# Turning the residual stream by DMA in the out projection instead of by TensorE in the feed-forward stage, with the feed-forward rounds in a new order

## The chip, the cores and the metric

The kernel runs on one core of a Trainium2 chip. The metric is device time in microseconds (us). The kernel before took 2558.52 us, the median of 3 runs (2558.04 to 2558.9). A profiled execution of it took 2555.83 us. A run with several rounds alternates both kernels on the same chip.

In what follows PE is TensorE, PEld its weight load, DVE is VectorE, ACT is ScalarE, POOL is GpSimd, and SP is SyncE, which here only issues transfers.

## The reference

A block of a transformer over 64 x 64 tokens with 1024 features, all in float32 but for two roundings to bfloat16. In short:

```python
# x: (64, 64, 1024); the second axis is the attention's sequence
y  = einsum("bct,bcd->bdt", x, cond_weights[itok_B_0_15])      # a 64x64 mix of positions per sequence
x1 = x + attention(y, qkvw, qkvb, ow, ob)                      # 32 heads of 32, softmax, out projection

base   = x1 @ W.T                                              # 1024 x 1024
logits = x1 @ Wr.T + 5 * one_hot(itok_B_0_7)                   # 8 experts
gates  = softmax over the two largest logits, 0 elsewhere
z      = base + 2 * sum over experts of gates * (x1 @ A.T) @ B.T    # LoRA of rank 16 per expert

q, s   = quantize(bf16(z) * inv)      # per token: s = max|.|/127, q = clip(round(./s), -127, 127)
inter  = bf16(clip(silu(gate) * up, -10, 10))    # gate, up: q @ w.T * s * w_scale, 512 wide
out    = x1 + (quantize(inter * inv_inter) @ w_down.T) * scales
```

Two products take x1: the router with the LoRA's first factor (8 x 17 = 136 columns), and the base (1024 columns). For a matmul on PE both need x1 with features on partitions, that is turned.

## The kernel before, in words

The 4096 tokens are 32 tiles of 128 tokens; two tiles make a pair, of which there are 16. The kernel has three stages in a row.

*Attention.* Eight blocks of four tiles. The order of work is written out by a small list of due times. Its result is stored per pair in DRAM (`ctx_d`), with features on partitions. In its last phase the first two pairs of the out projection are woven in.

*Out projection* (class `OutProjection`). For each pair, a product of 256 tokens x 1024 features with a 1024 x 1024 weight, by Winograd's variant of Strassen's scheme: seven products in place of eight, in the order 1, 6, 7, 5, 2, 4, 3. Each product is four float32 matmuls of 128 x 512, each issued as two instructions, so that one product is eight rows of the trace and about 3.43 us. `pair(p)` returns the seven steps; each has `product()` (the matmuls) and `rest()` (what reads the result). The PSUM banks are a, b, c, d: products 1 and 2 share a, 7 and 4 share c, 5 and 3 share d. `prepare(p + 1)` makes the four sums of token quarters (To, on DVE) for the next pair, after product 5. POOL adds the bias `ob` to the loaded x (L1092) and the shared sums `ou` (L1106). After product 3 SP stores the two tiles of x1 in the output tensor (L1114), then loads the context (`cx`, L1067) and x (`xo`, L1073) two pairs ahead. Each engine takes its instructions in the order in which they are written, and SP's transfers wait in one line as well: a transfer whose data is not ready holds up all after it.

*Feed-forward stage* (`second_stage`). One round per pair, in which pair p's router, base product and gates are computed, and the quantized gate, up and down products of pairs p-1 and p-2. The order within a round is written out by hand as a list of calls (`router`, `base(p, i)`, `after(p, i)`, `quant_a`, `quant_b`, `gate_or_up`, `scaled`, `glu`, `down`, `result`). Each round begins with `x1_transposed` (L1232, L1233): PE turns the sixteen 128 x 128 blocks of the pair's x1, which was loaded again from the output tensor (L1156), and ACT copies them from PSUM to SBUF. `quant_a` quantizes on DVE and ACT, `quant_b` clips and turns the bfloat16 values by a DMA transpose from SP (L1381). `result` adds the scaled down product to the output in DRAM by an accumulating transfer from POOL; only the last three tiles are added in SBUF, to an x1 that is still there, and stored.

The PSUM pool `ps_h` has four banks, taken in turn by `x1_transposed`, `router`, `down`, `gates_transposed` and `gate_or_up`; `ps_g` has four, for the products a to d.

Of the kernel before, what the change touches and what calls it, by code (L numbers as in the profile page):

```python
# [11 lines left out]
F32 = mybir.dt.float32  # L12
BF16 = mybir.dt.bfloat16
I32 = mybir.dt.int32
AF = mybir.ActivationFunctionType
# [4 lines left out]
P = 128  # L20
# [15 lines left out]
def adaln_attn_ffn(ctx: ExitStack, tc: tile.TileContext, a, out: bass.AP):  # L36
# [26 lines left out]

    I = a["w_gate_t"].shape[1]
# [9 lines left out]
    with tc.manual_schedule(), ExitStack() as psum, ExitStack() as early:  # L74
        ps_g = psum.enter_context(tc.tile_pool(name="ps_g", bufs=4, space=PSUM, reuse_waits="tile"))
        st = early.enter_context(tc.tile_pool(name="halve", bufs=2))
        chores = halve_weights(tc, st, const, dram, srcs, half, any_i)
        chores = itertools.chain(chores, combine_quarters(tc, st, (("wo", a["ow"]), ("wt", a["w_t"])), comb))
        op = OutProjection(tc, a, x_t, out_t, ctx_d, ps_g, comb, KC, H)
        attention(tc, a, x_t, ctx_d, ident, dram, ps_g, KC, PB, NBLK, NCH, HPC, H, C, chores, early, op)  # L80
        second_stage(tc, a, out_t, ident, ps_g, KC, NT, H, C, half, comb, op)

    inexact = nc.values_load(any_i[0:1, 0:1], min_val=0, max_val=1)
    with tc.If(inexact != 0):
        feed_forward(tc, a, x_t, out_t, ctx_d, ident, KC, NT, PB, H, C, None)

# [946 lines left out]
class OutProjection:  # L1033


    def __init__(self, tc, a, x_t, out_t, ctx_d, ps_g, comb, KC, H):
        self.tc, self.a, self.x_t, self.out_t, self.ctx_d, self.ps_g, self.comb = tc, a, x_t, out_t, ctx_d, ps_g, comb
        self.KC, self.H = KC, H
        self.NPAIR = len(ctx_d)
        self.stack = ExitStack()  # L1040
        self.st = {}
# [15 lines left out]
    def open_rest(self):  # L1057
        self.xp, self.tp, self.up = self.pool("xo3", 2), self.pool("to3", 2), self.pool("uo3", 1)
        self.load_x(0)
        self.load_ctx(1)  # L1060
        self.load_x(1)
        self.prepare(0)
# [17 lines left out]

    def pair(self, p):
# [5 lines left out]
        def one(i):  # L1087
# [8 lines left out]
            def rest():  # L1096
                x, ps = self.st[p]["x"], u.pop(("ps", i))
                if i in (1, 6, 7):
                    u[i] = self.up.tile([P, HH], F32, tag=f"u{i}", name=f"ou{i}_{p}")
                    if i == 1:  # L1100
                        nc.scalar.copy(u[1], ps)  # L1101
                    else:
                        nc.vector.tensor_tensor(u[i], ps, u[1 if i == 6 else 6], ALU.add)  # L1103
                    if i == 7:
                        for t, n, v in ((1, 1, u[7]), (0, 1, u[6]), (1, 0, u[6])):
                            nc.gpsimd.tensor_tensor(x[:, t, hs[n]], x[:, t, hs[n]], v, ALU.add)  # L1106
                    return
                t, n = {5: (1, 1), 2: (0, 0), 4: (0, 1), 3: (1, 0)}[i]
                nc.vector.tensor_tensor(x[:, t, hs[n]], ps, x[:, t, hs[n]], ALU.add)
# [14 lines left out]
def second_stage(tc, a, out_t, ident, ps_g, KC, NT, H, C, half, comb, op):  # L1124
# [12 lines left out]
    with ExitStack() as ctx:  # L1137
# [33 lines left out]
        for p in range(2, NPAIR):  # L1171
# [6 lines left out]
            if p == NPAIR - 3:  # L1178
                first_loads()
        op.stack.close()  # L1180
# [44 lines left out]
        def x1_transposed(p):  # L1225
            s = st[p]
            s["xT"] = p1p.tile([P, 2, KC, P], F32, tag="xT", name=f"xT_{p}")
            for t in range(2):
                for q in range(0, KC, 4):
                    ps = ps_h.tile([P, 4, P], F32, tag="h", name=f"xTp_{p}_{t}_{q}")  # L1230
                    for c in range(4):
                        nc.tensor.transpose(ps[:, c, :], s["x"][:, t, (q + c) * P:(q + c + 1) * P], ident)  # L1232
                    nc.scalar.copy(s["xT"][:, t, q:q + 4, :], ps)  # L1233
# [194 lines left out]
        def result(p, t, adds=None):  # L1428
# [3 lines left out]
            for n in range(2):  # L1432
# [3 lines left out]
                if adds:  # L1436
                    adds.tensor_add(y[:, hs[n]], y[:, hs[n]], s["x"][:, t, hs[n]])
# [11 lines left out]
        for p in range(NPAIR - 1):  # L1449
            q, r = p - 1, p - 2  # L1450
            old, last = q >= 0, r >= 0
            x1_transposed(p)
# [12 lines left out]
            do(old, quant_a, q, 0, "u")  # L1465
# [37 lines left out]
        x1_transposed(p)  # L1503
# [3 lines left out]
        quant_a(r, 1, "i")  # L1507
# [3 lines left out]
        quant_b(r, 1, "i")  # L1511
        base(p, 1)
        after(p, 1)
        route(p)
        result(r, 0)
        base(p, 6)
        gates_transposed(p)
# [112 lines left out]
```

## Time and profile before

| | |
|---|---|
| median of 3 runs | 2558.52 us (2558.04 to 2558.9) |
| the profiled execution | 2555.83 us |
| its span, first to last instruction | 2554.0 us |
| TensorE clock granted | 0.996 |
| attention, up to 1430 us | 1430 us, PE busy 1413.59 |
| attention's last phase with pairs 0 and 1, 1430 to 1487 us | 57 us, PE busy 55.26 |
| out projection, 1487 to 1830.4 us | 343.4 us, PE busy 343.40 |
| feed-forward, 1830.4 to 2554 us | 723.6 us, of which PE is idle mostly in the last 39 (busy 18.5) |

A row of the profile has the line, the engine, the operation, what it writes and reads (buffer numbers left out), and the number of instructions. In a timeline a row starts with the start in us from the span's start and the time that the row takes; a bracket at its end tells how long the engine was idle before and what it waited for. The number before "us to landing" of a transfer counts from its issue to its data's arrival. Times of matmuls are from issue to a modelled end, so that successive matmuls overlap in the table.

### The profile page before, as it was taken

How to read it: one execution, taken by the hardware profiler on the slowest of the kernel's cores; microseconds unless marked ns; L12 is line 12 of the kernel's file. 1: busy time of each engine (PE TensorE's matmuls, PEld its weight loads, DVE VectorE, ACT ScalarE, POOL GpSimd, SP SyncE). 2: the span in 40 equal slices, each digit the busy share in tenths (PEclk: the TensorE clock that was granted, in tenths of full speed). 3: DMA queues.
4: the chain of work that ended last, by engine and by line, in shares of the span. 5: the costliest groups of instructions: out<-in, count | busy, mean ns of one | idle time of the engine just before them, and what ended most of it. 6: DMA issues, size and time to landing. Idle time of an engine off the chain costs nothing.

```text
span 2554.0 us, 35008 instructions
## 1 busy us (share of the span) xinstructions
PE 2512.6 (98%) x13955; PEld 1779.0 (70%) x14000; DVE 1569.1 (61%) x2957; ACT 631.1 (25%) x1111; POOL 366.0 (14%) x451
## 2 busy tenths in 40 slices
PE   8999999999999999999999999999999999999996
PEld 7888888888888888888888644444454545455452
DVE  4575575674664655654745734434367777777777
ACT  1132231221221222322312200000033334343433
POOL 5110001011112221110000233434200000000001
PEclk9999999999999999999999999999999999999998
DMA  8664545555556546544443444443524344434333
GB/s 271 241 229 133 193 162 191 173 168 177 184 161 211 182 155 207 184 152 156 141 137 153 164 166 162 167 164 124 194 75 77 81 77 78 84 69 86 71 52 72
DMA packets 207885, 378.10 MB, mean 148 GB/s; under 512 B 96098, under 2 KB 150371, under 8 KB 196067
## 3 DMA queue, kind: packets, MB, share of 16 engines
q1 hardware_dynamic: 177202, 309.19, 37.1%
q0 software_dynamic: 12080, 49.82, 7.4%
q10 hardware_dynamic: 18432, 16.79, 1.9%
q8 instruction: 112, 1.84, 0.3%
q14 instruction: 59, 0.48, 0.1%
HBM read 271.40 MB, written 83.89 MB: 139 GB/s over the span
## 4 chain that ended last, share of the span: by engine, by line
PE 94%; DVE 3%; DMA 1%; ACT 0%; issue 0%; SPq 0%; DVEq 0%
PE pska L419 4%; PE pskd L419 4%; PE pskc L419 4%; PE psqa L419 4%; PE pod L995 4%; PE pbc L995 4%; PE pba L995 4%; PE psqd L419 4%; PE psvd L446 4%; PE psva L446 4%; PE psqc L419 4%; PE poa L995 4%; PE poc L995 4%; PE psvc L446 4%; PE pbd L995 4%; PE s L482 3%
## 5 line engine op out<-in xcount | busy, mean ns | idle before, releaser
L494 DVE TENSOR_REDUCE mx<-s 128x8 f32<-128x512 f32 x128 | 88.1, 689 | 138.5 <-PE s L482 137.4
L516 ACT COPY pT<-pt 128x512 f32<-128x512 f32 x128 | 75.0, 586 | 318.1 <-PE pt L514 318.1
L405 DVE SCALAR_TENSOR_TENSOR kbd<-pskd,bqkv,psku 32x256 f32<-32x256 f32 x256 | 122.8, 480 | 35.6 <-PE pskd L419 32.2
L536 ACT ACTIVATE co<-c,bqkv 128x256 f32<-128x256 f32 x128 | 60.6, 473 | 338.7 <-PE c L526 312.8
L1092 POOL TENSOR_TENSOR xo<-xo,ob 128x1024 f32<-128x1024 f32 x32 | 87.5, 2753 | 306.8 <-DMA xo<-in_x_dram 306.8
L419 PE MATMUL psqa<-yB,wq 128*128 128x256 f32 x512 | 123.5, 384 | 0.0
L419 PE MATMUL pska<-yB,wk 128*128 128x256 f32 x512 | 122.7, 383 | 0.0
L1441 POOL DMA_DIRECT2D out_dram<-y x29 | 25.1, 864 | 680.4 <-DVE y L1433 680.4
L446 PE MATMUL psva<-wv,yB 128*128 128x256 f32 x512 | 116.6, 381 | 0.0
L995 PE MATMUL poa<-woA,cx 128*128 128x512 f32 x256 | 115.3, 593 | 0.0
L995 PE MATMUL pba<-wtA,xT 128*128 128x512 f32 x256 | 115.1, 592 | 0.0
L498 ACT ACTIVATE prob<-prob 128x512 f32<-128x512 f32 x128 | 78.9, 628 | 108.1 <-DVE prob L495 81.5
L446 PEld LDWEIGHTS psva<-wv,yB 128*128 128x128 f32 x512 | 96.1, 190 | 12.9
L419 PEld LDWEIGHTS pska<-yB,wk 128*128 128x128 f32 x512 | 94.1, 190 | 12.2
L419 PEld LDWEIGHTS psqa<-yB,wq 128*128 128x128 f32 x512 | 92.8, 190 | 12.0 <-issue 0.2
L1106 POOL TENSOR_TENSOR xo<-xo,ou 128x512 f32<-128x512 f32 x48 | 59.4, 1266 | 249.4 <-DVE ou L1103 249.4
L506 DVE TENSOR_TENSOR prob<-prob,den 128x512 f32<-128x512 f32 x128 | 91.0, 711 | 4.4
L405 DVE SCALAR_TENSOR_TENSOR kbd<-pskc,bqkv,psku 32x256 f32<-32x256 f32 x128 | 61.5, 481 | 51.3 <-PE pskc L419 49.9
L495 DVE TENSOR_TENSOR prob<-s,mx 128x512 f32<-128x512 f32 x128 | 88.5, 691 | 4.4
L504 DVE TENSOR_REDUCE den<-prob 128x8 f32<-128x512 f32 x128 | 86.6, 677 | 7.0 <-ACT prob L498 6.8
L1101 ACT COPY ou<-poa 128x512 f32<-128x512 f32 x16 | 9.4, 585 | 327.1 <-PE poa L995 326.7
L995 PEld LDWEIGHTS poa<-woA,cx 128*128 128x128 f32 x256 | 48.4, 190 | 59.9 <-issue 59.8
(244 smaller groups left out, 5276.9 us busy)
## 6 DMA issues: line engine op xcount, KB each, us to landing
wv<-v_d SPq DMA_DIRECT2D x98, 512.0 KB, 3.7
wq<-q_d SPq DMA_DIRECT2D x28, 1792.0 KB, 7.9
wk<-k_d SPq DMA_DIRECT2D x28, 1792.0 KB, 8.0
x<-in_x_dram SPq DMA_DIRECT2D x32, 512.0 KB, 9.7
ctx_d<-co ACTq DMA_DIRECT2D x128, 128.0 KB, 5.6
cx<-ctx_d SPq DMA_DIRECT2D x16, 1024.0 KB, 5.9
xo<-in_x_dram SPq DMA_DIRECT2D x32, 512.0 KB, 5.2
out_dram<-xo SPq DMA_DIRECT2D x32, 512.0 KB, 2.7
```

Of the source, the lines that this page charges most:

```text
L405: nc.vector.scalar_tensor_tensor(dst, ps, bias, u, ALU.add, ALU.add)
L419: nc.tensor.matmul(ps[:, 0:HB], A[:, SLOT[A_OF[i]], k, :], B[B_OF[i]][:, k, :], start=first and k == 0, stop=k == KQ - 1, skip_group_check ...
L446: nc.tensor.matmul(ps[:, j * VC:(j + 1) * VC], B[B_OF[i]][:, k, j * P:(j + 1) * P], A[:, k, :], start=first and j == 0 and k == 0, stop=k ...
L482: nc.tensor.matmul(ps[halves[r], hp, n, jj * 2:(jj + 1) * 2, :], q_of[b, c][halves[hp], m, t * HB + t0:t * HB + t0 + C], kbd[u][halves[hp] ...
L494: nc.vector.tensor_reduce(mx_v, ps, AX.X, ALU.max)
L495: nc.vector.tensor_tensor(p.rearrange("p (a e) k -> p a e k", a=2), ps, mx_v.unsqueeze(3).to_broadcast([P, 2, HPC, C]), ALU.subtract)
L498: nc.scalar.activation(p, p, AF.Exp, scale=scale)
L504: nc.vector.tensor_reduce(den, p, AX.X, ALU.add)
L506: nc.vector.tensor_tensor(p, p, den.unsqueeze(2).to_broadcast([P, n, C]), ALU.mult)
L516: nc.scalar.copy(pT, pt)
L995: self.nc.tensor.matmul(ps, self.B[self.B_OF[i]][:, k, :], self.A[self.A_OF[i]][:, k, :], start=first and k == 0, stop=k == self.KQ - 1, s ...
L1092: nc.gpsimd.tensor_add(s["x"][:, t, :], s["x"][:, t, :], self.ob)
```

## The change

*In the out projection* each finished tile of x1 is turned in the shadow of the other work. [...]`turn(p, t)` has ACT split half a tile (512 features of float32) into its two 16-bit planes (`planes`, a view of the words as low and high halves), and SP turns both planes with one DMA transpose. `turned()`, called later, has ACT weave the turned planes back into float32, and SP stores that in a new DRAM tensor `xT_d[p]`. Tile 0 is turned after product 4 and woven back after product 3; tile 1 is turned after product 3, and woven back after product 6 of the next pair (for the last pair at the stage's end).

*In the feed-forward stage* `x1_transposed` is gone; `load_x1` loads the turned pair as one transfer of 1 MB, at the head of the round before. The last three tiles' x1 is loaded from the output tensor at the head of the last round.

*The rounds' order:* the token sums move ahead of the inner activation's `quant_a`; its `quant_b` moves into the next `quant_a`; `gates_transposed` moves behind product 5, and the first gate product moves ahead of the LoRA matmul of product 5. In the last round product 7 follows product 6.

```diff
+def planes(x):
+    return x.bitcast(I16).rearrange("p (n h) -> p h n", h=2)
...
 class OutProjection:
...
     def open_rest(self):
         self.xp, self.tp, self.up = self.pool("xo3", 2), self.pool("to3", 2), self.pool("uo3", 1)
+        self.hp = self.pool("ho3", 2)
...
+    def turn(self, p, t):
+        nc, n = self.tc.nc, self.H // 2
+        for f in range(2):
+            h = self.hp.tile([P, 2, n], I16, tag="h", name=f"xh_{p}_{t}_{f}")
+            nc.scalar.copy(h, planes(self.st[p]["x"][:, t, f * n:(f + 1) * n]))
+            hT = self.hp.tile([P, 2, n], I16, tag="hT", name=f"xhT_{p}_{t}_{f}")
+            nc.sync.dma_start(
+                hT.rearrange("p h (k q) -> p (h k) q", q=P), h.rearrange("p h n -> p (h n)"), transpose=True
+            )
+            self.turning.append((p, t, f, hT))
+
+    def turned(self):
+        nc, n, KQ = self.tc.nc, self.H // 2, self.KC // 2
+        for p, t, f, hT in self.turning:
+            xT = self.hp.tile([P, KQ, P], F32, tag="xT", name=f"xTo_{p}_{t}_{f}")
+            nc.scalar.copy(planes(xT.rearrange("p k q -> p (k q)")), hT)
+            nc.sync.dma_start(self.xT_d[p][:, t, f * KQ:(f + 1) * KQ, :], xT)
+        self.turning = []
...
             def rest():
                 x, ps = self.st[p]["x"], u.pop(("ps", i))
+                if i in (6, 3):
+                    self.turned()
...
                 if i == 5 and p + 1 < self.NPAIR:
                     self.prepare(p + 1)
+                if i in (4, 3):
+                    self.turn(p, t)
                 if i == 3:
                     for t in range(2):
                         nc.sync.dma_start(self.out_t[2 * p + t], x[:, t, :])
...
         def load_x1(p):
             s = st1[p] = {}
-            s["x"] = xp1.tile([P, 2, H], F32, tag="x", name=f"x1_{p}")
-            for t in range(2):
-                nc.sync.dma_start(s["x"][:, t, :], out_t[2 * p + t])
+            s["xT"] = xp1.tile([P, 2, KC, P], F32, tag="x", name=f"x1T_{p}")
+            nc.sync.dma_start(s["xT"], xT_d[p])
...
+        op.turned()
         op.stack.close()
...
-        def x1_transposed(p):
-            s = st[p]
-            s["xT"] = p1p.tile([P, 2, KC, P], F32, tag="xT", name=f"xT_{p}")
-            for t in range(2):
-                for q in range(0, KC, 4):
-                    ps = ps_h.tile([P, 4, P], F32, tag="h", name=f"xTp_{p}_{t}_{q}")
-                    for c in range(4):
-                        nc.tensor.transpose(ps[:, c, :], s["x"][:, t, (q + c) * P:(q + c + 1) * P], ident)
-                    nc.scalar.copy(s["xT"][:, t, q:q + 4, :], ps)
-            s["B"] = token_quarters(s["xT"], KQ)
-
         def token_sums(p):
             s = st[p]
+            s["B"] = token_quarters(s["xT"], KQ)
...
         for p in range(NPAIR - 1):
             q, r = p - 1, p - 2
             old, last = q >= 0, r >= 0
-            x1_transposed(p)
+            do(p > 0, load_x1, p + 1)
             do(old, after, q, 3)
             do(last, scaled, r, 1, "u")
             do(last, glu, r, 1)
-            do(last, quant_a, r, 1, "i")
             router(p)
             do(last, down, r, 0)
-            do(p + 2 < NPAIR, load_x1, p + 2)
             token_sums(p)
-            do(last, quant_b, r, 1, "i")
+            do(last, quant_a, r, 1, "i")
             base(p, 1)
             after(p, 1)
             do(last, result, r, 0)
-            do(old, quant_a, q, 0, "u")
+            do(old, quant_a, q, 0, "u", (r, 1, "i") if last else None)
             base(p, 6)
             route(p)
             after(p, 6)
             do(old, quant_b, q, 0, "u")
             base(p, 7)
             do(last, down, r, 1)
-            gates_transposed(p)
             do(last, result, r, 1)
             base(p, 5)
+            gates_transposed(p)
             do(old, quant_a, q, 1, "g")
+            do(old, gate_or_up, q, 0, "g")
             lora_5(p)
             after(p, 7)
             after(p, 5)
-            do(old, gate_or_up, q, 0, "g")
...
         p, q, r = NPAIR - 1, NPAIR - 2, NPAIR - 3
-        x1_transposed(p)
+        st[q]["x", 1] = p1p.tile([P, H], F32, tag="xl", name="x1_l")
+        nc.sync.dma_start(st[q]["x", 1], out_t[2 * q + 1])
+        xl = xp1.tile([P, 2, KC, P], F32, tag="x", name="x1_ll").rearrange("p t k n -> p t (k n)")
+        for t in range(2):
+            st[p]["x", t] = xl[:, t, :]
+            nc.sync.dma_start(xl[:, t, :], out_t[2 * p + t])
...
         base(p, 6)
+        base(p, 7)
         gates_transposed(p)
         after(p, 6)
         quant_a(q, 0, "u")
         base(p, 2)
         after(p, 2)
+        after(p, 7)
         quant_a(q, 1, "g", (q, 0, "u"))
         down(r, 1)
         result(r, 1)
-        base(p, 7)
-        after(p, 7)
```

More of the change, by code (lines that the diff above doesn't have):

```diff
@@ L14 @@
 I32 = mybir.dt.int32
+I16 = mybir.dt.int16
 AF = mybir.ActivationFunctionType
@@ L61, in adaln_attn_ffn @@
     ]
+    xT_d = [dram.tile([P, 2, KC, P], F32, tag=f"xT_d{p}", name=f"xT_d{p}") for p in range(NT // 2)]
     I = a["w_gate_t"].shape[1]
@@ L78, in adaln_attn_ffn @@
         chores = itertools.chain(chores, combine_quarters(tc, st, (("wo", a["ow"]), ("wt", a["w_t"])), comb))
-        op = OutProjection(tc, a, x_t, out_t, ctx_d, ps_g, comb, KC, H)
+        op = OutProjection(tc, a, x_t, out_t, ctx_d, xT_d, ps_g, comb, KC, H)
         attention(tc, a, x_t, ctx_d, ident, dram, ps_g, KC, PB, NBLK, NCH, HPC, H, C, chores, early, op)
-        second_stage(tc, a, out_t, ident, ps_g, KC, NT, H, C, half, comb, op)
+        second_stage(tc, a, out_t, xT_d, ident, ps_g, KC, NT, H, C, half, comb, op)
     inexact = nc.values_load(any_i[0:1, 0:1], min_val=0, max_val=1)
@@ L1033, with __init__ @@
 class OutProjection:
-    def __init__(self, tc, a, x_t, out_t, ctx_d, ps_g, comb, KC, H):
+    def __init__(self, tc, a, x_t, out_t, ctx_d, xT_d, ps_g, comb, KC, H):
         self.tc, self.a, self.x_t, self.out_t, self.ctx_d, self.ps_g, self.comb = tc, a, x_t, out_t, ctx_d, ps_g, comb
+        self.xT_d, self.turning = xT_d, []
         self.KC, self.H = KC, H
@@ L1121, in pair, with second_stage @@
         return [one(i) for i in Winograd.ORDER]
-def second_stage(tc, a, out_t, ident, ps_g, KC, NT, H, C, half, comb, op):
+def second_stage(tc, a, out_t, xT_d, ident, ps_g, KC, NT, H, C, half, comb, op):
     nc = tc.nc
@@ L1436, in result @@
                 if adds:
-                    adds.tensor_add(y[:, hs[n]], y[:, hs[n]], s["x"][:, t, hs[n]])
+                    adds.tensor_add(y[:, hs[n]], y[:, hs[n]], s["x", t][:, hs[n]])
                     nc.sync.dma_start(out_t[2 * p + t, :, hs[n]], y[:, hs[n]])
@@ L1506, in second_stage @@
         glu(r, 1)
-        quant_a(r, 1, "i")
         router(p)
@@ L1510, in second_stage @@
         token_sums(p)
-        quant_b(r, 1, "i")
+        quant_a(r, 1, "i")
         base(p, 1)
@@ L1514, in second_stage @@
         route(p)
+        quant_b(r, 1, "i")
         result(r, 0)
         base(p, 6)
+        base(p, 7)
         gates_transposed(p)
```

## The prediction

> **What bounds the kernel now.** I read the page's busy shares and its chain of work first, then the busy time by stage, then the timeline of one feed-forward round and of one out-projection pair.
>
> ```profile
> PE 2512.6 (98%) x13955; PEld 1779.0 (70%) x14000; DVE 1569.1 (61%) x2957; ACT 631.1 (25%) x1111; POOL 366.0 (14%) x451
> ...
> PE 94%; DVE 3%; DMA 1%; ACT 0%; issue 0%; SPq 0%; DVEq 0%
> ```
>
> TensorE (PE) works 98% of the span and is 94% of the chain that ended last: time taken off PE's list is time off the end, unless something new makes PE wait. By stage (columns: stretch, length, then busy time of PE, PEld, DVE, ACT, POOL, clock, DMA share, GB/s):
>
> ```profile
> 1487.00:1830.40 343.40, 343.40 (x802) 152.11 (x801) 152.87 (x141) 8.20 (x14) 128.82 (x72) 1.00 0.41 152
> 2122.00:2471.80 349.80, 348.54 (x1289) 181.77 (x1312) 269.82 (x578) 133.44 (x186) 13.77 (x16) 1.00 0.39 76
> 2515.00:2554.00 39.00, 18.50 (x75) 7.25 (x73) 28.44 (x54) 12.94 (x17) 6.34 (x5) 0.75 0.28 70
> ```
>
> The out projection (first line) has PE busy all the time and ACT nearly idle. In the feed-forward stage (second line) PE idles 1.26 us in eight rounds; DVE is at 77%. Only the last 39 us belong to a DVE and ACT chain. The head of one feed-forward round:
>
> ```profile
> 2122.23 1.91 PE L1232 MATMUL xTp<-ident,x 128*128 128x128 f32 x16
> 2122.87 2.05 ACT L1233 COPY xT<-xTp 128x512 f32<-128x512 f32 x4 [1.65 <-PE xTp L1232]
> 2123.98 3.87 PE L1246 MATMUL pr<-awr,xT 128*128 128x136 f32 x32
> ```
>
> From the first turning matmul to the first router matmul is 2123.98 - 2122.23 = 1.75 us of PE's list. The 1.91 us holds the pipelined end of the last matmul, which hides under the router.
>
> **What the skill says.** The Trainium skill, "TensorE: Matmul & The Clock Gate", Part 4: PE-mode transpose, gives about 275 ns for one 128x128 turn and says the result goes to PSUM, so a copy follows. The trace agrees (273 ns, four copies), but shows that the price in a stream is the spacing, 1.75/16 = 0.11 us, not the latency. "DMA: Bandwidth & Descriptors", DMA Transpose (X-bar), Constraints: 2-byte types only, into SBUF. That is why float32 is split into two 16-bit planes; the transposes of bf16 in this trace have the same number of 16-bit words. "SBUF — State Buffer", Who interferes with whom: DVE and GpSimd share a port pair as an exclusive lock. The trace agrees: sums To take 2.72 and 2.83 us beside POOL's adds, 0.69 us without. The same page, Door 1: The DMA port swizzle, says that a 2-byte operand may stride up to 8 elements at full bandwidth (the planes stride 2); no row here shows a strided 16-bit copy on ACT.
>
> **The change, part by part.** *Removed on PE:* 16 rounds x 16 matmuls at 1.75 us = 28.0 us. In round 1 the router also waited for the ACT copies (1863.95 to 1866.31 = 2.36 us in place of 1.75), so 28.6 us. ACT's four copies per round (2.05 us) go too, but ACT was not the bound.
>
> *Added on ACT and the queues, per out-projection pair:* 8 ACT copies of 128x1024 16-bit words, 4 DMA transposes, 4 stores of 256 KB. Nearest rows: a 128x1024 ACT cast takes 1.06 us, and the transposes of the same word count:
>
> ```profile
> L1370 ACT ACTIVATE qb_g<-q_g x32: 1056/1057/1057, 1864.7 to 2518.0; 128x1024 bf16<-128x1024 f32 x32
> L1381 SPq DMA_TRANSPOSE qT_g<-qb_g x32: 1232/1233/1467, 1866.3 to 2519.6; - x32
> ...
> DMA to landing us min/median/max: 3.0/3.0/5.0
> ```
>
> ACT: 8 x 1.06 = 8.5 us of a pair's 24.03. SP: 4 x 1.23 + 4 x 0.34 = 6.3 us. I take 1.06 and 3.0; the copies' ends are 0.5 (a plane read at double rate) and 2.12 (a stride that halves it), the landing's 3.0 and 5.0. No DVE or PE instruction is added here. What stands behind the new waits matters:
>
> ```profile
> 1653.14 1.00 DVE L1005 TENSOR_TENSOR To<-cx 128x512 f32<-128x512 f32 x1
> 1653.55 5.56 POOL L1092 TENSOR_TENSOR xo<-xo,ob 128x1024 f32<-128x1024 f32 x2
> 1654.18 2.72 DVE L1006 TENSOR_TENSOR To<-cx,To 128x512 f32<-128x512 f32 x1
> ...
> 1660.78 0.68 DVE L1109 TENSOR_TENSOR xo<-poc,xo 128x512 f32<-128x512 f32 x1
> 1661.49 2.42 SPq L1114 DMA_DIRECT2D out_dram<-xo  x2
> 1662.58 3.60 PE L995 MATMUL poa<-woA,cx 128*128 128x512 f32 x8
> ...
> 1663.96 0.42 SPq L1067 DMA_DIRECT2D cx<-ctx_d  x1
> ```
>
> Call E the pair's end (1662.58, where the next pair's first product starts) and D4 the end of the add on poc (1661.46). SP's order becomes: two transposes (tile 0), two stores (tile 0), two transposes (tile 1), two out stores, then the load of cx two pairs ahead, then x. So the cx load, now at E+1.4, waits for: two copies 2.1, second landing 3.0 plus 0.1, its copy back 1.06, two copies of tile 1 2.1, a transpose's issue 1.23, two stores 0.7, all from D4: D4+10.4. With 5.9 us to land (median of cx) it is there at D4+16.3, which is E+15.2. The sums To of that pair start at E+14.6 today (1677.18 - 1662.58). They start some 0.6 us later, but POOL's 5.56 us, waiting for x (issued after the out stores' 2.7 us, landing 5.2 us later: about E+17), begins after most of them, so they take 2.8 to 4.9 us instead of 7.1. PE needs the add on poa done by the next pair's start, E+24.03: 15.2 + 4.9 + 0.7 = E+20.8. Cost on PE: nothing, with 3.2 us of cover. The loop from D4 to the next D4 is 16.3 + 4.9 + 1.3 = 22.5 us against PE's 24.03; with the old 7.1 us of sums it would be 24.7.
>
> Other instructions queued behind ACT's new waits: the copy of poa to ou, from E+3.6 to about E+7. DVE's sum on pob needs it at E+7.1, and the PE product that reuses the bank of poa comes at E+13.7. Hidden. In the last attention phase two such pairs run beside scores; the copies co and ou move some 2.4 us, with the same kind of cover.
>
> *At the stage's border:* the last store of turned tiles and the loads of ig, iu, wg and so on go out some 9 us later. ig is first used about 29 us into the stage, so hidden. ACT is held until about E+10.5 by the last turned copies; the gates are then ready near E+14, and PE turns them at E+17.5. But in round 0 nothing lies between that turn and the LoRA matmul now: turn to result plus gT copy is 0.78 us (1846.57 to 1847.35), of which 0.2 is covered. Cost 0.6 us.
>
> *Rounds in a new order:* the same instructions. Sums T now precede quantization of the inner activation; the down product needs its transpose at 15.7 us into the round (2139.71 - 2123.98) and has it at 12.8. The second half of that down product takes the PSUM bank of the router, free once gh is read at about 15.5; PE comes at 16.6. Turning the gates after the fifth product is covered by the gate product (1.75 us against 0.78). All cost nothing; the bank is the thinnest cover, 1.1 us, and without it each microsecond costs 14 in all.
>
> *The end:* the last 39 us hang on DVE from the sum on pbd (a PE wait of 1.57 us before it), so they move with PE. Three x tiles are loaded from out a round ahead.
>
> Sum: -28.6 + 0.6 = -28.0 us. The profiled execution, span 2554.0 and 2555.83 us in all (1.83 around the span), becomes 2526.0 and 2527.8. The median of the runs is 2558.52, 2.7 above the profiled one: 2530.5.
>
> **Rivals.** *A, the feed-forward order makes PE wait* (the router's bank, or a transpose landing at 5.0): up to 1 us in each of 14 rounds, gain 14: 2544. For it: the 1.1 us of cover. Against: DVE's list up to gh has the same length as before. Chance 0.11. *B, the out-projection loop passes 24.03 a little:* at the old 7.1 us of sums it is 24.7, 0.7 x 14 pairs = 10 us back: 2540. For it: POOL's lock is visible today. Against: x arrives after cx. Chance 0.07. *C, slower:* 16-bit strided copies at 2.12 us. Five copies lie between D4 and the cx load, so +5.3, the loop 22.5 + 5.3 = 27.8 us, 3.8 x 14 = 53 us lost: 2530.5 + 53 = 2583. It decides from a loop of 26.0 us (2 x 14 = 28 eaten); 26.4 makes it 0.2% slower. For it: no row of that kind. Against: ACT's rate is the same for all its 128x1024 rows (1.01 to 1.15 us), whatever the type. Chance 0.05. *D, no net change*, the loop near 26.0: 0.02. The forecast keeps 0.75, with a range of its own of 2527 to 2534.
>
> **How the numbers follow.** Some 0.2% (5 us) is what a measurement can tell from none. Faster: forecast 0.75, A 0.11, B 0.07, so 0.93; same: D 0.02; slower: C 0.05. The range leaves out C, D and the worse parts of A and B: 2526 to 2541.
>
> **What would show it.** Right: no xTp; the feed-forward round at 41.75 us where it is 43.5 (from 2122.23 to 2470.26 are eight rounds: 348.03 / 8); out-projection pairs at 24.03; sums To shorter than 2.7 us each; ACT about 8.5 us busier per pair; a PE wait of about 0.6 us in round 0 at the LoRA matmul. Wrong: PE waits on xo or To adds in the out projection, cx landing after E+19, copies xh or xTo far from 1.06 us, or PE waits on gh or qT_i in each round.

## The result and the profile after

The changed kernel took 2530.22 us (median of 4 runs, 2530.07 to 2531.45), beside 2558.28 us (2557.47 to 2558.9, 4 runs) for the kernel before: 28.06 us less, a ratio of 0.9892 with a 95% interval of 0.9874 to 0.9909. The profiled execution took 2530.18 us, its span is 2528.4 us.

From the page of the changed kernel, the busy shares and the shares of the chain of work that ended last:

```profile
PE 2487.7 (98%) x13744; PEld 1752.1 (69%) x13744; DVE 1525.9 (60%) x2957; ACT 742.1 (29%) x1175; POOL 360.6 (14%) x451
...
PE 95%; DVE 4%; issue 0%; ACT 0%; DMA 0%; SPq 0%; DVEq 0%
```

PE is busy for 24.9 us less (2512.6 to 2487.7), and ACT for 111 us more (631.1 to 742.1). The bound is the same. Busy time by stage (stretch, length, then PE, PEld, DVE, ACT, POOL, clock, DMA share, GB/s):

```profile
1488.00:1831.80 343.80, 343.80 (x803) 152.20 (x802) 112.73 (x140) 138.75 (x129) 125.31 (x72) 1.00 0.77 239
1900.00:2444.00 544.00, 544.00 (x1904) 272.04 (x1903) 433.75 (x938) 187.45 (x249) 22.64 (x26) 1.00 0.41 82
2489.00:2528.40 39.40, 18.52 (x72) 7.28 (x70) 27.89 (x53) 12.96 (x17) 6.34 (x5) 0.71 0.28 69
```

In the out projection ACT goes from 8.20 us to 138.75 us of work and the DMA share from 0.41 to 0.77, and PE is still busy in all of the 343.80 us. DVE falls from 152.87 to 112.73 us there, mostly because in nearly every pair at least three of the four sums To now run clear of POOL. From 1900 to 2444 us, in the feed-forward stage, PE has no idle time. Two router products eight rounds apart, from the timeline:

```profile
2110.97 3.87 PE L1272 MATMUL pr<-awr,x1T 128*128 128x136 f32 x32
...
2444.98 3.87 PE L1272 MATMUL pr<-awr,x1T 128*128 128x136 f32 x32
```

A round takes (2444.98 - 2110.97) / 8 = 41.75 us, where it was 43.50. What the turning costs on the other engines, from the rows by tile (ns at least, in the median and at most):

```profile
L1098 ACT COPY xh<-xo x64: 1032/1044/1053, 1466.8 to 1835.5; 128x1024 int16<-128x1024 int16 x64
L1109 ACT COPY xTo<-xhT x64: 1321/1337/1356, 1470.9 to 1839.8; 128x1024 int16<-128x1024 int16 x64
L1100 SPq DMA_TRANSPOSE xhT<-xh x64: 1231/1234/2441, 1467.9 to 1836.9; - x64
DMA to landing us min/median/max: 2.7/2.7/4.5
```

And PE's waits after 1400 us (us in total, times, longest):

```profile
PE qTp_u L1411 <- DVE qb_u L1404: 7.2, 1, 7.2
PE qTp_i L1411 <- DVE qb_i L1404: 5.0, 2, 2.8
...
PE pbd L1337 <- ACT gT L1334: 0.5, 1, 0.5
PE pu L1421 <- DMA qT_u<-qb_u: 0.2, 1, 0.2
```

The first two lie in the tail and were there before. The third is the forecast one of round 0. None concerns the turned data or the out projection. One of its pairs, from the timeline:

```profile
1663.56 3.60 PE L1004 MATMUL poa<-woA,cx 128*128 128x512 f32 x8
1671.71 0.83 SPq L1079 DMA_DIRECT2D cx<-ctx_d  x1
1678.50 0.69 DVE L1014 TENSOR_TENSOR To<-cx 128x512 f32<-128x512 f32 x1 [0.26 <-DMA cx<-ctx_d]
1680.43 2.83 DVE L1017 TENSOR_TENSOR To<-cx,To 128x512 f32<-128x512 f32 x1
1683.19 0.68 DVE L1143 TENSOR_TENSOR xo<-poa,xo 128x512 f32<-128x512 f32 x1
1684.43 0.69 DVE L1143 TENSOR_TENSOR xo<-poc,xo 128x512 f32<-128x512 f32 x1 [0.56 <-PE poc L1004]
1687.59 3.60 PE L1004 MATMUL poa<-woA,cx 128*128 128x512 f32 x8
```

The pair still takes 24.03 us (1663.56 to 1687.59), though the load of cx now leaves 8.15 us after the pair's end instead of 1.4, and DVE waits for its landing (0.26 us here).

**Where the 25.6 us between the two spans lie** (2554.0 to 2528.4; the first PE instruction of the feed-forward stage is the mark):

| stretch | us |
|---|---|
| up to the stage's first PE instruction (1830.81 to 1831.79) | +0.98 |
| from there to the first of the last round (639.45 to 613.19) | -26.26 |
| the last round's own turning | -1.74 |
| from the last router product to the end | +1.4 |

The second and third are the change's. Of the first, a full microsecond is already there when the first pair begins, inside attention, which the change doesn't touch; in another execution of the same changed kernel the mark lies at 1829.49. The fourth begins after the 7.2 us wait, with products that take 3.56 and 3.60 us where the trace of before has 2.97 and 2.67; in the other execution it is +0.7, and the second stretch is 613.19 us again. The profiled execution of before was 2.5 us quicker than that kernel's median here and that of after equals its own, so the medians differ by 28.06.

### The profile page after: what moved, and what is told of

Same layout as the page of the kernel before. It is cut to its first block, busy times and chain, and to the rows that moved or that the text cites. A ratio compares the mean times of both kernels' runs of the same rounds, so it can differ in the third digit from the quotient of the medians.

```text
span 2528.4 us, 34876 instructions
## 1 busy us (share of the span) xinstructions
PE 2487.7 (98%) x13744; PEld 1752.1 (69%) x13744; DVE 1525.9 (60%) x2957; ACT 742.1 (29%) x1175; POOL 360.6 (14%) x451
## 4 chain that ended last, share of the span: by engine, by line
PE 95%; DVE 4%; issue 0%; ACT 0%; DMA 0%; SPq 0%; DVEq 0%
PE pska L428 4%; PE psvd L455 4%; PE pskd L428 4%; PE pskc L428 4%; PE psqa L428 4%; PE pod L1004 4%; PE pbc L1004 4%; PE pba L1004 4%; PE psqd L428 4%; PE psva L455 4%; PE psqc L428 4%; PE psvc L455 4%; PE poa L1004 4%; PE poc L1004 4%; PE pbd L1004 4%; PE s L491 3%
## 5 line engine op out<-in xcount | busy, mean ns | idle before, releaser
L1124 POOL TENSOR_TENSOR xo<-xo,ob 128x1024 f32<-128x1024 f32 x32 | 81.7, 2574 | 341.7 <-DMA xo<-in_x_dram 334.7
L1004 PE MATMUL pba<-wtA,x1T 128*128 128x512 f32 x256 | 115.1, 592 | 0.0
L1098 ACT COPY xh<-xo 128x1024 int16<-128x1024 int16 x64 | 64.7, 1043 | 159.2 <-DVE xo L1143 159.2
L1109 ACT COPY xTo<-xhT 128x1024 int16<-128x1024 int16 x64 | 84.6, 1338 | 57.7 <-DMA xhT<-xh 53.0
```

Source lines behind the costliest of these rows:

```text
L1004: self.nc.tensor.matmul(ps, self.B[self.B_OF[i]][:, k, :], self.A[self.A_OF[i]][:, k, :], start=first and k == 0, stop=k == self.KQ - 1, s ...
L1109: nc.scalar.copy(planes(xT.rearrange("p k q -> p (k q)")), hT)
L1124: nc.gpsimd.tensor_add(s["x"][:, t, :], s["x"][:, t, :], self.ob)
```

## The experiments

My theory: PE's list is the time. 16 x 1.75 us of turning leave it, what replaces them hides in the out projection, and the new order is worth nothing by itself. The rivals: the order carries part of the gain; the turning costs something that the gain has paid for; the covers that the prediction counted are not there. On the chips of these runs the kernel before took 2555.1 to 2555.9 us, so ratios are compared, not times across chips.

### The order alone, the turning alone, and no turning

Three kernels. The first keeps PE's turning and takes the rounds' new order:

```diff
         for p in range(NPAIR - 1):
...
             router(p)
             do(last, down, r, 0)
             token_sums(p)
-            do(last, quant_b, r, 1, "i")
+            do(last, quant_a, r, 1, "i")
...
             base(p, 5)
+            gates_transposed(p)
             do(old, quant_a, q, 1, "g")
+            do(old, gate_or_up, q, 0, "g")
             lora_5(p)
```

> The kernel before with the rounds in the new order alone; TensorE still turns x1 at the head of each round, the out projection is untouched. The theory (the gain is the 16 x 1.75 us of turning matmuls and nothing else) expects no change: within 2 us of 2558.3. The rival, that the new order takes waits away and so carries part of the gain, expects a gain of 3 us or more here, and the same amount missing in the run of the turning alone.

The second is the changed kernel with the rounds in the order of before.

> The changed kernel with the rounds in the old order: the turning by DMA alone. The theory expects the whole gain, with the 0.6 us of round 0 not lost, as product 5 again lies between the gates' turn and the LoRA matmul: 28.6 us, 2529.7. The rival, that the old order would make TensorE wait once the turning matmuls are gone, expects 2533 or more, with TensorE waiting on gh or gT in each round.

The third, in the new order, leaves the turning out: nothing is split or turned, and the feed-forward stage loads x1 as it lies, so that its products are made of unturned rows.

```diff
-                if i in (6, 3):
-                    self.turned()
...
-                if i in (4, 3):
-                    self.turn(p, t)
...
-            nc.sync.dma_start(s["xT"], xT_d[p])
+            for t in range(2):
+                nc.sync.dma_start(s["xT"][:, t, :, :].rearrange("p k q -> p (k q)"), out_t[2 * p + t])
...
-        op.turned()
```

> The changed kernel without any turning in the out projection (no copies on ACT, no DMA transposes, no stores of the turned planes); the feed-forward stage loads x1 unturned in its place, so the residual stream enters the router and the base product in a wrong layout. This measures the price of the turning itself. The theory, that it is hidden, expects the changed kernel's time: 2529 to 2531.5, out-projection pairs at 24.03 us in both. A rival, that contention of the added transfers and copies costs something, expects this run at least 3 us below the changed kernel.

| kernel | us (runs) | ratio to before, 95% interval |
|---|---|---|
| before, same chip | 2555.07 (2553.15 to 2557.3) | |
| order alone | 2555.86 (2554.4 to 2558.33) | 1.0004 (0.9995 to 1.0012) |
| turning alone | 2527.82 (2526.35 to 2527.91) | 0.9893 (0.9877 to 0.991) |
| new order, no turning | 2526.29 (2524.72 to 2528.41) | 0.989 (0.9873 to 0.9906) |

The order alone gives nothing, and the turning alone has the whole ratio of the changed kernel. With all of the turning's copies and transfers taken out, the ratio is the same within its interval: what replaces PE's work is hidden, to within the 2 us or so that these medians resolve. The trace is finer. In this kernel the out projection takes as long as the changed kernel's 343.80 us, with ACT at 8.20 us and the DMA share at 0.40:

```profile
1485.15:1828.97 343.82, 343.82 (x803) 152.19 (x802) 152.83 (x141) 8.20 (x14) 128.79 (x72) 1.00 0.40 151
```

Two of PE's waits with the order alone:

```profile
PE pbd L1311 <- ACT gT L1308: 0.5, 1, 0.5
PE pr L1246 <- ACT xT L1233: 0.4, 1, 0.4
```

The 0.5 us of round 0 comes with the order, as the prediction argued; the kernel without any turning has it too. But the old order with the turning does not save it. It has this wait, in round 0 only, and before it DVE's first step towards the gates starts late:

```profile
PE ghp L1332 <- DVE gh L1319: 0.6, 1, 0.6
...
1838.68 0.17 DVE L1288 TENSOR_TENSOR lg<-pr,bias 128x16 f32<-128x16 f32 x1 [4.70 <-ACT xTo L1109]
```

There the gates themselves come 0.6 us too late for PE: DVE stands 4.70 us until ACT has woven the last turned planes back. So with the turning round 0 loses about as much in either order, once to the order and once to the turning (32.12 us from router to router in the new order, 32.16 in the old), and the two orders cannot be told apart by time.

### How thin the covers are: the copies twice

The prediction's slower rival needs turning copies of twice the price. Here both kinds are made twice, so that ACT has 9.5 us more per pair:

```diff
-            nc.scalar.copy(h, planes(self.st[p]["x"][:, t, f * n:(f + 1) * n]))
+            for _ in range(2):
+                nc.scalar.copy(h, planes(self.st[p]["x"][:, t, f * n:(f + 1) * n]))
...
-            nc.scalar.copy(planes(xT.rearrange("p k q -> p (k q)")), hT)
+            for _ in range(2):
+                nc.scalar.copy(planes(xT.rearrange("p k q -> p (k q)")), hT)
```

> The changed kernel with each of the eight 16-bit copies on ACT made twice, as if a strided copy took double. In the changed kernel's trace the add on poc to the issue of the cx load is 10.6 us, the load's landing 6.8, the sums To 4.8 and two adds 1.3: 23.5 us against 24.03 of TensorE. Five of the doubled copies lie in that chain (1.04 + 2 x 1.34 + 2 x 1.04 = 5.8 us), so the theory, that the loop over the cx load bounds the stage once it passes 24.03, expects some 29.3 us per pair, 5.2 x 13 pairs = 68 us more than the changed kernel: about 2598, and TensorE waiting at the first product of each pair. If ACT's idle time hides the copies after all, the time stays at 2530.

Measured: 2592.39 us (2589.49 to 2594.96), ratio 1.0143 (1.0127 to 1.016). Scaled by the ratio of 0.9892 the changed kernel would be at 2527.5 on this chip, so the cost is 65 us. The largest of the new waits of PE:

```profile
PE poa L1004 <- ACT ou L1137: 39.8, 14, 9.2
```

The size is near the 68 us of the expectation's ring of waits, and above the 53 us of the prediction's slower rival. The instruction that PE waits for is not the forecast one: it is ACT's copy of the first product (ou<-poa), which frees the bank of poa, and which the prediction had called hidden by several microseconds. That left open whether ACT's own queue or the ring of waits through SP sets the pace.

### Only the first copy twice, and then the cx load moved

Doubling only the split copy xh adds 4 x 1.04 = 4.2 us per pair. I expected ACT's queue alone to matter, with room to spare:

> Only the copy xh<-xo that splits a half tile into planes is done twice, so ScalarE has 4 x 1.04 = 4.2 us more in a pair of the out-projection loop, where doubling both copies gave 9.5 us more and 4.2 us of waits a pair. Theory (TensorE waits only once ScalarE's copy ou<-poa, queued behind the turning copies, comes too late, so a cover of about 5.3 us a pair must be used up first): loop at 24.0 us, no wait on ou, the changed kernel's time within 3 us. Rival (every added microsecond of ScalarE comes out as a wait in the same share as in the doubled version, 4.2 of 9.5): 1.9 us a pair, 14 pairs, 26 us slower than the changed kernel.

Measured: 2560.2 us (2555.35 to 2567.65), ratio 1.0019 (1.0012 to 1.0025), and 31.4 us more than the changed kernel on the same chip (2528.79, below). My theory fell; the rival's number is nearer, but it names no mechanism. The timeline of one pair shows it, with SP, DVE, ACT and PE in order of time:

```profile
1664.45 0.83 SPq L1079 DMA_DIRECT2D cx<-ctx_d  x1
1671.03 0.69 DVE L1014 TENSOR_TENSOR To<-cx 128x512 f32<-128x512 f32 x1 [4.84 <-DMA cx<-ctx_d]
1673.57 0.68 DVE L1144 TENSOR_TENSOR xo<-poa,xo 128x512 f32<-128x512 f32 x1
1674.34 4.14 ACT L1099 COPY xh<-xo 128x1024 int16<-128x1024 int16 x4 [8.11 <-DVE xo L1144]
1680.37 2.53 ACT L1110 COPY xTo<-xhT 128x1024 int16<-128x1024 int16 x2 [1.88 <-DMA xhT<-xh]
1682.77 4.13 ACT L1099 COPY xh<-xo 128x1024 int16<-128x1024 int16 x4
1684.90 3.25 SPq L1101 DMA_TRANSPOSE xhT<-xh  x2
1686.81 0.58 ACT L1136 COPY ou<-poa 128x512 f32<-128x512 f32 x1
1687.43 3.70 PE L1004 MATMUL poa<-woA,cx 128*128 128x512 f32 x8 [0.56 <-ACT ou L1136]
1689.30 0.83 SPq L1079 DMA_DIRECT2D cx<-ctx_d  x1
```

It is a ring. The load of cx lands 6.6 us after its issue; DVE has stood 4.84 us at the sums To, and the adds into xo, whose products were long done, stand behind them; ACT stands 8.11 us for the adds, then has its copies; SP's transposes wait for these; and the next load of cx is behind them in SP's queue. From load to load: 1689.30 - 1664.45 = 24.85 us, longer than the 24.03 us that PE needs. The copy ou<-poa comes late only because the ring pushes all of ACT's list back. In the mean over the 13 pairs after the one at 1494.38, a pair takes 25.3 us here, and counted likewise 27.7 us with both copies doubled (29.3 were expected there).

If that is so, taking cx out of the ring must give the time back, with ACT's doubled copies left as they are:

```diff
             def rest():
                 x, ps = self.st[p]["x"], u.pop(("ps", i))
+                if i == 3 and p + 2 < self.NPAIR:
+                    self.load_ctx(p + 2)
                 if i in (6, 3):
                     self.turned()
...
                     if p + 2 < self.NPAIR:
-                        self.load_ctx(p + 2)
                         self.load_x(p + 2)
```

> The copy xh<-xo is done twice as in the run before, with the load of cx moved ahead of the turning transfers in SP's queue. Theory (what slowed the doubled version is the ring of the prediction: cx load behind the turning transfers on SP, then the sums To, then DVE's adds queued behind them, then the copies xh on ACT, then SP again; it was 24.9 us in the steady pairs): with cx out of the ring the sums To wait for nothing, the loop is 24.0 us again, no wait on ou, and the time is within 4 us of the changed kernel, ratio to the kernel before about 0.99. Rival (ACT's own queue is the cause: four copies of 4.1 us stand ahead of the copy ou<-poa whatever SP does): the time stays near 2560, ratio about 1.002, with the waits on ou as before.

Measured: 2528.69 us (2527.25 to 2530.34), ratio 0.9897 (0.9881 to 0.9914), where the ratio without the move was 1.0019. From the timeline of this kernel:

```profile
1661.63 0.57 SPq L1079 DMA_DIRECT2D cx<-ctx_d  x1
...
1668.78 0.58 ACT L1138 COPY ou<-poa 128x512 f32<-128x512 f32 x1
...
1674.36 3.60 PE L1004 MATMUL poa<-woA,cx 128*128 128x512 f32 x8
1675.22 1.01 DVE L1014 TENSOR_TENSOR To<-cx 128x512 f32<-128x512 f32 x1
```

The load leaves 1.0 us after the pair's end (1660.63), the sums wait for nothing, ACT's copy ou is done 5.0 us before product 2 wants the bank (1669.36 against 1674.36), and pairs take 24.03 us with no wait of PE in the loop. So the cost of the doubled copy xh came through the ring, and none that the runs resolve from ACT's load. With both copies doubled the move was not tried; that the same ring is at work there is argued from the same wait on ou. Nor was the move tried in the changed kernel itself, where PE already waits for nothing in these pairs and no gain in time is to be expected.

### The thinnest cover of the feed-forward rounds

The token sums T are made twice, four sums more on DVE ahead of the quantization and the gates:

```diff
-            sums_of_tokens(nc.vector, T, s["B"])
+            for _ in range(2):
+                sums_of_tokens(nc.vector, T, token_quarters(s["xT"], KQ))
+            sums_of_tokens_views(T, s["B"])
...
```

> The changed kernel with the token sums T of each feed-forward round made twice: 2.7 us more on DVE ahead of the router's results. It prices the thinnest cover that the prediction named: gh is ready 15.5 us into the round, TensorE takes the router's PSUM bank for the second half of a down product at 16.6. The theory expects gh at 18.2 and TensorE to wait 1.6 us there in each of 13 rounds: 21 us more, 2551. The rival, that DVE's eight idle microseconds per round take the work, expects 2530.

Measured: 2545.05 us (2543.83 to 2547.85), ratio 0.9959 (0.9944 to 0.9973), beside 2555.34 us for before; some 17 us more than the changed kernel's ratio gives there (2527.7). PE's largest wait:

```profile
PE pd L1456 <- DMA qT_i<-qb_i: 16.4, 13, 2.0
```

The wait comes once a round, 16.4 / 13 = 1.26 us. The second set of sums makes the transpose of the inner activation, qT_i, leave 2.52 us later (12.19 us after the round's first router product, where the changed kernel has 9.67), so a cover of about 2.52 - 1.26 = 1.3 us was used up. The changed kernel shows it directly: the transpose's issue, its time to landing, and the product that needs it, in the round whose router starts at 2194.47:

```profile
2204.14 1.57 SPq L1407 DMA_TRANSPOSE qT_i<-qb_i  x1
...
qT_i<-qb_i SPq DMA_TRANSPOSE x1, 4.9
...
2210.20 1.89 PE L1450 MATMUL pd<-wd,qT_i 128*128 128x512 bf16 x8
```

It lands at 2204.14 + 4.9 = 2209.0, 1.2 us before PE comes. The router's PSUM bank has hardly more: gh has been read 15.15 us into the round, and the second half of this product takes the bank at 16.6, so 1.4 us. With the doubled sums the wait for qT_i stands ahead of the bank on PE and hides it, so this run does not tell what the bank alone would cost.

### A further turn moved from PE to DMA

By the same exchange the gates gh, two matmuls a round, can go. First version: split on ACT, one DMA transpose, woven back on ACT, with the LoRA matmul of product 5 after product 2 in the rounds where no older pair gives cover:

```diff
+        def gates_turn(p):
...
+            h = p1p.tile([P, 2, 2 * P], I16, tag="gp", name=f"gp_{p}")
+            nc.scalar.copy(h, planes(gh.rearrange("p t n -> p (t n)")))
+            hT = s["gpT"] = p1p.tile([P, 2, 2 * P], I16, tag="gpT", name=f"gpT_{p}")
+            nc.sync.dma_start(
+                hT.rearrange("p h (k q) -> p (h k) q", q=P), h.rearrange("p h n -> p (h n)"), transpose=True
+            )
...
-            ps = ps_h.tile([P, 2, P], F32, tag="h", name=f"ghp_{p}")
...
-            for t in range(2):
-                nc.tensor.transpose(ps[:, t, :], gh[:, t, :], ident)
...
-            nc.scalar.copy(s["gT"], ps)
+            nc.scalar.copy(planes(s["gT"].rearrange("p t n -> p (t n)")), s.pop("gpT"))
...
```

> The changed kernel with the gates too turned by DMA: ACT splits gh into 16-bit planes after the routing, SP turns them, ACT weaves them back where the gates' turn stood; in round 0 the LoRA matmul of product 5 moves behind product 2. It carries the theory one step on: TensorE's list loses 2 matmuls and their bank, 0.23 us in 16 rounds (3.7 us), and the wait of 0.5 us in round 0. The chain is 0.5 + 2.5 + 0.7 us, gT at about 20 us of the round, needed at 22.6, so 4 us less than the changed kernel: 2526. If the added transpose holds up the next one on SP, or gT is late, the time is 2530 or more.

Measured: 2538.88 us (2537.93 to 2539.29), ratio 0.9935 (0.9921 to 0.9948): slower than the changed kernel. Its timeline in round 0:

```profile
1850.91 2.47 SPq L1333 DMA_TRANSPOSE gpT<-gp  x1
...
1862.91 0.76 ACT L1340 COPY gT<-gpT 128x512 int16<-128x512 int16 x1 [12.65 <-DMA gpT<-gp]
1863.73 2.07 PE L1343 MATMUL pba<-bm,gT 128*128 128x512 f32 x2 [10.82 <-ACT gT L1340]
```

In round 0 this small transpose is issued right behind the loads of the stage's weights and lands some 12 us later; in the other rounds it lands in 2.4. The last of these loads, issued 1.3 us before it, takes 12.8 us to land. PE stands 10.8 us.

A second attempt at the end of the kernel gives PE 28 matmuls whose result nobody reads in the 7.2 us wait, against the slow matmuls after it:

```diff
...
         glu(q, 1)
+        warm(28)
         quant_b(p, 1, "u", True)
```

> The changed kernel with 28 idle matmuls (6 us of work whose result nothing reads) in the gap of 7.18 us in which TensorE waits for DVE near the end. After that gap eight matmuls take 3.56 us in place of 1.89, and granted clock in the last 39 us is 0.71. If the gap is what lowers the clock, the matmuls after it run at full speed: 1 to 2.5 us less, 2528 to 2529. If the last products hang on DVE and ACT whatever the clock is, nothing changes: 2530.

Measured: 2529.3 us (2527.41 to 2529.45), ratio 0.9898 (0.9883 to 0.9914), no change that the runs resolve. PE in the tail, without and then with these matmuls:

```profile
2498.70 3.56 PE L1421 MATMUL pg<-wg,qT_g 128*128 128x512 bf16 x8
```

```profile
2496.67 1.89 PE L1421 MATMUL pg<-wg,qT_g 128*128 128x512 bf16 x8
...
2509.45 3.60 PE L1450 MATMUL pd<-wd,qT_i 128*128 128x512 bf16 x8 [0.68 <-ACT qT_i L1412]
```

The product after the gap now takes 1.89 us, as elsewhere in the stage, but after the next gap (4.11 us) a product is slow again. From the last router product to the end this kernel takes 82.27 us, two traces of the changed kernel 83.42 and 82.72. Most of the last 36 us is DVE's and ACT's in both, 23.3 and 10.8 us here, 23.6 and 10.8 without these matmuls. Both attempts together:

> The gates by DMA and the idle matmuls together. If both theories hold the gains add up: 2524 to 2525, some 34 us below the kernel before. If neither does: 2530.

Measured: 2537.72 us (2537.12 to 2541.39), ratio 0.9931 (0.9918 to 0.9945), the first version's result.

The last version keeps PE's turn of the gates in round 0, where the weight loads are ahead in the queue, and uses the DMA in rounds 1 to 15. Against the first version:

```diff
         def gates_turn(p):
+            if p == 0:
+                return
...
         def gates_transposed(p):
+            if p == 0:
+                ps = ps_h.tile([P, 2, P], F32, tag="h", name=f"ghp_{p}")
+                gh = s.pop("gh")
+                for t in range(2):
+                    nc.tensor.transpose(ps[:, t, :], gh[:, t, :], ident)
+                nc.scalar.copy(s["gT"], ps)
-            nc.scalar.copy(planes(s["gT"].rearrange("p t n -> p (t n)")), s.pop("gpT"))
+            else:
+                nc.scalar.copy(planes(s["gT"].rearrange("p t n -> p (t n)")), s.pop("gpT"))
```

> The gate rows of rounds 1 to 15 are turned by DMA through int16 planes instead of two TensorE matmuls; round 0, where that transfer sat 12 us in SP's queue behind the weights, keeps TensorE's turn, and its LoRA product for the fifth block comes after the second block's product. Theory (TensorE's own work is the time, and only round 0 spoiled the first version): 15 rounds lose 0.22 us each and round 0 its wait of 0.46, so 3.8 us below the changed kernel, ratio to the kernel before 0.9876 (about 0.9985 of the changed kernel); rounds at 41.53 us and no wait on gT. Rival (ScalarE's two more copies of about 0.8 us a round, or the later gates, cost elsewhere what TensorE saves): the time of the changed kernel within 1 us, with a wait of TensorE on gT or on an activation's transpose in the rounds.

The changed kernel was timed beside it:

> The changed kernel itself, timed again on the same chip as the two kernels beside it. Ratio to the kernel before 0.989 (0.9875 to 0.9905) by either theory.

| kernel | us (runs) | ratio to before, 95% interval |
|---|---|---|
| before, same chip | 2555.94 (2554.2 to 2559.06) | |
| the changed kernel again | 2528.79 (2527.18 to 2529.69) | 0.9894 (0.9878 to 0.9911) |
| gates by DMA but in round 0 | 2525.13 (2524.86 to 2526.53) | 0.988 (0.9864 to 0.9897) |

It is 3.7 us below the changed kernel, with 3.8 expected. The intervals against before overlap, so I lean on the trace. From its timeline, round 0 and two router products eight rounds apart:

```profile
1848.90 0.43 PE L1346 MATMUL ghp<-ident,gh 128*128 128x128 f32 x2 [0.29 <-DVE gh L1319]
...
2108.65 3.87 PE L1272 MATMUL pr<-awr,x1T 128*128 128x136 f32 x32
...
2440.92 3.87 PE L1272 MATMUL pr<-awr,x1T 128*128 128x136 f32 x32
```

A round is (2440.92 - 2108.65) / 8 = 41.53 us, 0.22 less, and round 0 waits 0.29 us in place of 0.46. From the first router product to the last it is 609.92 us, where the changed kernel timed with it has 613.19: 3.27 us by the trace, and the last round's 0.22 to come.

## Why the prediction was right

The forecast was 2530.5 us, the median is 2530.22, by the forecast's own mechanism. That the two meet within 0.3 us is in part luck, as the sum below shows. Step by step:

- **PE's turning, -28.0 us.** Right: the round went from 43.50 to 41.75 us, and the turning alone gives the whole ratio. The extra time of round 1, forecast as 0.6, went too: that round is 2.47 us shorter (40.77 to 38.30), 0.72 beyond the turning's 1.75.
- **Round 0, +0.6.** Right in place, a little small in size: the wait is 0.46, but counted by the round's length, which went from 33.14 to 32.12 us instead of 31.39, it is 0.73. It cancels against round 1. That it belongs to the new order is only half right: with the turning, the old order pays as much at the gates instead.
- **The price of a strided 16-bit copy, bounded by 0.5 and 2.12, taken as 1.06.** Mis-sized for one half, without effect. The copy that reads with a stride of two (xh) takes 1.04, the one that writes so (xTo) 1.34. Rival C fell with this. The landing was taken as 3.0 and is 2.7; that of cx as 5.9 and is 6.6.
- **The covers in the out projection.** In the pair shown above, with its E at 1663.56, cx was forecast to be there at E+15.2 and the sums To start at E+14.9; they were to take 2.8 to 4.9 us and take 4.8; the add on poa was to be done by E+20.8 and is by E+20.3. The ring was put at 22.5 us, a cover of 1.5. A single turn between two cx loads does not measure it, since they are uneven: after the load at 1671.71 the turns are 24.86 and 22.57 us. In the long one POOL's adds fall on one of the sums To, and DVE stands 0.56 us for PE; in the short one the sums take 2.6 us, and DVE stands longer:

```profile
1708.46 0.69 DVE L1143 TENSOR_TENSOR xo<-poc,xo 128x512 f32<-128x512 f32 x1 [2.06 <-PE poc L1004]
```

Without these waits for PE the two turns would be 24.3 and 20.5 us, 22.4 in the mean: an estimate from this trace, near the forecast. A turn above 24.03 does no harm when the next makes it up. So PE never waits, but not by much.
- **Rival C's price of a longer ring.** "It decides from a loop of 26.0 us" was a little high. With only xh doubled, pairs of 25.3 us already end 0.2% behind the kernel before. The term mis-sized is the cost, taken as the excess of each pair alone. From the pair at 1469.06 to the stage's end (1856.14) this kernel takes 25.3 us more than the changed kernel (1470.01 to 1831.79). The 13 pairs with their excess of 1.29 us make 16.8 of it; the other 8.5 lie in the last pair, which takes 32.56 us (1823.58 to 1856.14). There the transposes stand behind the loads for the next stage in SP's queue, PE waits, and the product after the wait is slow as well, 6.49 us instead of 3.6:

```profile
1825.12 3.60 SPq L1203 DMA_DIRECT2D lang_i<-in_lang_dram  x2
...
1842.95 6.49 PE L1004 MATMUL poa<-woA,cx 128*128 128x512 f32 x8 [5.48 <-ACT ou L1136]
```

- **ACT's copy ou<-poa, hidden.** Right in the changed kernel: done at E+5.8 (1669.39) and wanted at E+13.7. It only fails once the ring has gone round too slowly.
- **The rounds' order, nothing.** Right: 1.0004 alone. One cover was mis-sized, without effect: the inner activation's transpose has 1.2 us where the prediction had 2.9. It was to be there 12.8 us into the round and is at 14.6, because its landing takes 4.9 us in this place and not the 3.0 that the forecast took; in the old order (the turning alone) it mostly takes 2.4, with the order alone 4.9. The router's bank, named as the thinnest with 1.1, has 1.4. What slows the landing was not settled.
- **The sum.** Forecast for the spans -28.0, measured -25.6, because attention took 1.0 and the tail 1.4 us longer in that one execution; in the later profiled execution of the same kernel the span is 2525.4 us, 28.6 below before. The forecast of the median holds to 0.3 us since the 2.7 us between the profiled execution and the median of before was added on, and in the changed kernel that distance is nil: the span is missed by 2.4 us and the distance by 2.7, and the two cancel. The ratio is the better test: 2530.5 / 2558.52 = 0.9890 was forecast, and 0.9892, and in the later runs 0.9894, were measured. What makes up the tail's 1.4 us was not settled: products after its gaps differ from trace to trace, and keeping PE at work there gave nothing that the runs resolve.

## What to carry to other kernels

When PE is busy all the time, work that DMA and an idle engine can do comes off one for one, even if they need five times as long for it: here 1.75 us of PE a pair became 9.5 us of ACT and four DMA transposes. Before trusting it, follow each new wait around the queues until it comes back to where it began: a load that stands behind it in SP's queue closes a ring, and what counts is the ring's length against PE's period, not the busy share of any engine. If it is near, move the load ahead of the waiting transfers; and use a small transfer's usual landing only where nothing large has been queued before it. Nor does a usual landing hold when the transfer moves in the order of work: here one went from 2.4 to 4.9 us.

## What the hardware showed that I had not expected

- A copy on ACT of 128x1024 16-bit words costs 28% more when it writes every second word (1.34 us) than when it reads so (1.04 us). The Trainium skill, "SBUF — State Buffer", Door 1: The DMA port swizzle, lets a 2-byte operand stride up to 8 elements at full bandwidth; the read agrees (a cast of the same shape takes 1.06 us), the write does not. For the gates, 128x512 words, the two copies take 0.62 and 0.77 us.
- The same DMA transpose of the gates that lands in 2.4 us took 12 us behind the stage's weight loads.
- After a gap of some 7 us eight matmuls took 3.56 us (2.97 in the trace of before), and 1.89 us when PE had been kept busy in the gap.
